# Neighbourhood attention on one core: softmax sums from columns of ones beside the values, two heads to a bank, in the slot of the logits

## The chip, the cores and the metric

The kernel runs on one core of a Trainium2 chip. The metric is the device time in microseconds (us) of one execution. TensorE (PE in the profile; PEld for its weight loads) multiplies matrices into banks of PSUM; VectorE (DVE), ScalarE (ACT) and GpSimd (POOL) work on elements; SyncE (SP) issues the DMA transfers. Every engine works through its own queue of instructions, and semaphores hold one engine back for another.

## The reference, cut to what matters

The input x is 4 images of 128 channels and 64 x 64 pixels. The program is a layer 0 and a layer 1; the change is in the attention of layer 0. Cut to what matters:

```python
y = layernorm_over_channels(x); y = y + depthwise_conv3x3(y)
# windows of 16 x 16 pixels: 64 of them; 2 branches, 4 heads of 32 channels
q, k, v = Wq @ y, Wk @ y, Wv @ y                 # per window, branch and head
logits = q . k over the 5 x 5 neighbours of each pixel * 32 ** -0.5
attn = softmax(logits)                           # out-of-window neighbours are zeros: logit 0, value 0
x = x + (Wo[0] @ o[0] + 0.5 * Wo[1] @ o[1]) / rect      # o = attn-weighted sum of v
# layer 1, over 4096 tokens of 128 channels
t = t + causal_linear_attention(layernorm(t))
t = t + recurrence(layernorm(t))                 # y_t = sigmoid(BN(W x)_t + V y_(t-1))
```

The softmax needs, for each query, a sum of exponentials of its logits (with a constant added for neighbours outside the window, `pad_c`), and the sum of values weighted by these exponentials. Their quotient is o.

## The kernel before

The image is cut into 16 bands of 16 rows (4 in each of 4 images), a band into 4 windows, so there are 64 windows, `places`. A loop runs over 66 slots. Slot i computes the logits of window i and has six gaps, 0 to 5, into which pieces of two other jobs are put by `between(i, gap)`: one step of `behind` (layer 1 of an earlier band: a list of 24 steps, `order`, one a gap over four slots, begun in slot 4m+5 for band m) and one step of `ahead` (`front()`: layer norm and depthwise convolution of the next band; in a slot that opens a band only in gaps 0, 2 and 4). `in_order()` fixes each engine's instructions in the order in which the code writes them, so that a waiting instruction holds up everything later on its engine.

What a slot holds, by lines of the profile:

- `logits` (L377, L382): four banks, one a head. Masks are added by a bf16 product. The keys of a head lie on 32 partitions, so four heads run in four row tiles of the array. ACT then writes four tiles of exponentials, `es` (L391, 128 keys by 512 queries of both branches).
- `weighted`, for the window of the slot before: (L400) for each head a product of 128x32 ones with `es`, on column tiles of 32, gives the sums in 128 rows of a bank; ACT copies them (`den`, L403), a DMA folds four rows into a 128x16 tile `dc` (L405). (L412) 24 products of values (128 keys by 32 channels) and a span of `es`, over 2 branches and 3 blocks of rows, give the weighted values of four heads in one bank; ACT copies them (`o_sb`, L420). DVE adds the constant and takes reciprocals (L423, L425); they go to DRAM (`rd`, L429) and come back broadcast over the 32 channels of each head (`rden`, L431).
- `window_inputs`, for the next window: q, k (L337) and v (L350) from `y2w`, the convolved half band of two windows; ACT copies each. v is needed with three different sets of 128 keys; the middle one is put together by two DMAs (L359, L360).
- `scaled`, for the window before last: POOL multiplies `o_sb` by `rden` into `oT` (L440), which `output0` of layer 1 multiplies by Wo (L465).

The order in a slot is: logits(i), gap 0, scaled(i-2), sums of window i-1, gap 1, values of i-1, gap 2, reciprocals, q of i+1, gap 3, k, gap 4, v, gap 5.

`convolve` gives `y2w` for two windows: ACT makes the first tap (L286), DVE the other eight (L288), ACT copies the result into window order (L324). In `front()` this copy for the first half of band n+1 falls in gap 0 of slot 4n+3, that for the second half in gap 0 of slot 4n+4. (In the first band it is made earlier by three steps.)

Tiles in a pool with one buffer (`p1`) can't be written again before their last reader is done; pools `p2` and `p3` have two and three buffers. PSUM's eight banks are used in turn.

After the 66 slots the rest of layer 1 runs out, and the recurrence follows as a chain of 43 steps (L771 to L823).

Of the kernel before, what the change touches and what calls it, by code (L numbers as in the profile page):

```python
# [9 lines left out]
F32 = mybir.dt.float32  # L10
# [7 lines left out]
P = 128  # L18
# [3 lines left out]
NB = H // WS  # L22
WT = WS * WS
# [23 lines left out]
def conv_attn_hybrid(ctx: ExitStack, tc: tile.TileContext, ins: dict, out: bass.AP):  # L47
    nc = tc.nc
# [100 lines left out]
    for i in range(2):  # L149
        t = const.tile([P, 4, P + 1], F32, name=f"v1_{i}")  # L150
        nc.vector.memset(t, 1.0)
        v1s.append(t)

    stats = const.tile([P, B * T // 512, 6], F32, name="stats")

# [20 lines left out]
    def bank():  # L176
        return ps.tile([P, 512], F32, tag="bank", name="bank")

    def run(g):
        for _ in g:  # L180
            pass
# [148 lines left out]
    def window_inputs(w, n, wj):  # L330


        y2 = y2s[n, wj // 2][:, wj % 2, :]
        for name, wT in (("q", wqT), ("k", wkT)):
            pps = bank()
            for br in range(BR):
                nc.tensor.matmul(  # L337
                    pps[:, br * WT : (br + 1) * WT],
                    wT[:, br * P : (br + 1) * P],
                    y2,  # L340
                    start=True,
                    stop=True,
                )
            w[name] = p2.tile([P, BR * WT], F32, tag=name, name=name)
            nc.scalar.copy(w[name], pps)  # L345
            yield
        vps = bank()
        v_sb = p2.tile([P, 3, BR * P], F32, tag="v_sb", name="v_sb")
        for e in range(2):
            nc.tensor.matmul(  # L350
                vps[:, e * 256 : (e + 1) * 256],
                y2[:, e * P : (e + 1) * P],
                wvT,
                start=True,
                stop=True,
            )
        nc.scalar.copy(v_sb[:, 0::2, :], vps.rearrange("p (e t) -> p e t", e=2))  # L357

        nc.sync.dma_start(v_sb[:64, 1, :], v_sb[64:, 0, :])  # L359
        nc.sync.dma_start(v_sb[64:, 1, :], v_sb[:64, 2, :])  # L360
        w["v"] = v_sb
        yield

    pieces = [(br, n) for br in range(BR) for n in range(len(BLOCKS))]
# [1 line left out]
    def spans(br, n):  # L366
        r0, r1, key0 = BLOCKS[n]
        return slice(br * WT + r0 * WS, br * WT + r1 * WS), br * WT + key0 * WS

    def logits(w):  # L370


        sps = [bank() for _ in range(HEADS)]
        for h in range(HEADS):
            rows = slice(h * HD, (h + 1) * HD)

            nc.tensor.matmul(sps[h], mask_k[rows], mask_q[rows], start=True, stop=False)  # L377
        for br, n in pieces:
            cols, k0 = spans(br, n)
            for h in range(HEADS):  # L380
                rows = slice(h * HD, (h + 1) * HD)
                nc.tensor.matmul(  # L382
                    sps[h][:, cols],
                    w["k"][rows, k0 : k0 + P],
                    w["q"][rows, cols],
                    start=False,
                    stop=(br, n) == pieces[-1],
                )
        for h in range(HEADS):
            es = p2.tile([P, BR * WT], F32, tag=f"es{h}", name=f"es{h}")  # L390
            nc.scalar.activation(es, sps[h], AF.Exp, scale=scale)  # L391
            w["es", h] = es

    def weighted(w):


        ops, dps = bank(), bank()
        for h in range(HEADS):
            rows = slice(h * HD, (h + 1) * HD)
            nc.tensor.matmul(dps[rows], ones[:, :HD], w["es", h], start=True, stop=True)  # L400

        den = p1.tile([P, BR * WT], F32, tag="den", name="den")
        nc.scalar.copy(den, dps)  # L403
        dc = p2.tile([P, 16], F32, tag="dc", name="dc")
        nc.sync.dma_start(dc, den[::HD, :])  # L405
        yield
        for br, n in pieces:
            cols, _ = spans(br, n)
            for h in range(HEADS):
                rows = slice(h * HD, (h + 1) * HD)  # L410
                c0 = br * P + h * HD
                nc.tensor.matmul(  # L412
                    ops[rows, cols],
                    w["v"][:, n, c0 : c0 + HD],
                    w["es", h][:, cols],
                    start=(br, n) == pieces[0],
                    stop=(br, n) == pieces[-1],
                )
        o_sb = p2.tile([P, BR * WT], F32, tag="o_sb", name="o_sb")
        nc.scalar.copy(o_sb, ops)  # L420
        yield

        nc.vector.tensor_tensor(dc, dc, pad_c, ALU.add)  # L423
        rc = p2.tile([P, 16], F32, tag="rc", name="rc")
        nc.vector.reciprocal(rc, dc)  # L425
        nc.vector.tensor_tensor(dmax, dmax, dc, ALU.max)
        nc.vector.tensor_tensor(dmin, dmin, dc, ALU.min)
        rd = dram4.tile([HEADS, BR * WT], F32, tag="rd", name="rd")
        nc.sync.dma_start(rd.rearrange("h (a e) -> (h a) e", e=16), rc)  # L429
        rden = p1.tile([P, BR * WT], F32, tag="rden", name="rden")  # L430
        nc.sync.dma_start(rden, rd.unsqueeze(1).to_broadcast([HEADS, HD, BR * WT]))  # L431
        w["o"], w["rden"] = o_sb, rden
        yield

# [173 lines left out]
    def layer1(n, last):  # L608

        a, c = Half(n, 0), Half(n, 1)  # L610
        y, z = last
        order = [
            (keep, z), None,
            (norm, z), (product, y), None,
            (output0, a), (measure, a), None,
            (turn_last, z), None,
            (norm, a), (output0, c), (measure, c), None,
            (turn, a), None,
            (product, z), (norm, c), None,
            (queries, a), None,  # L620
            (keys, a), None,
            (turn, c), None,
            (values, a), None,
            (queries, c), None,
            (scores, a), None,
            (keys, c), None,
            (turn_keys, a), None,
            (values, c), None,
            (accumulate, a), None,
            (turn_keys, c), None,  # L630
            (attend, a, 0), None,
            (attend, a, 1), (measure, a), None,
            (scores, c), (keep, a), None,
            (accumulate, c), (norm, a), None,
            (attend, c, 0), None,
            (turn_last, a), (attend, c, 1), (measure, c), None,
        ]
        for what in order:
            if what is None:
                yield  # L640
            elif what[1] is not None:
                what[0](*what[1:])
        halves[n] = a, c
# [17 lines left out]
    def front():  # L661


        for n in range(1, len(bands)):
            yield from norm_rows(n)
            if bands[n][1]:
                yield
            yield from convolve(n, 0)
            yield
            if n == 1:  # L670

                for _ in range(3):
                    yield
            yield from convolve(n, 1)
# [12 lines left out]
    windows = {0: {}}  # L687
    run(window_inputs(windows[0], 0, 0))
    run(third)
    ahead, behind = front(), iter(())  # L690

    def between(i, gap):


        next(behind, None)
        if i < len(places) and (i == 0 or i % NB or gap in (0, 2, 4)):
            next(ahead, None)

    for i in range(len(places) + 2):
        if i < len(places):  # L700
            n, wj = places[i]
            if i and wj == 0 and n + 1 < len(bands) and bands[n + 1][1] < NB - 1:
                load_head(n + 2)
            logits(windows[i])
        if 2 <= i:
            m, wjm = places[i - 2]
            if wjm == NB - 1:
                run(behind)
                behind = layer1(m, halves.pop(m - 1, (None, None)))
        between(i, 0)  # L710
        if 2 <= i:
            scaled(m, wjm, windows.pop(i - 2))
        if i < len(places) and wj == 1 and n + 2 < len(bands):
            load(n + 2)
        sums = weighted(windows[i - 1]) if 1 <= i <= len(places) else iter(())
        for gap in (1, 2):
            next(sums, None)
            between(i, gap)
        run(sums)
        if i == 0:  # L720
            run(fourth)
        inputs = iter(())
        if i + 1 < len(places):
            windows[i + 1] = {}
            inputs = window_inputs(windows[i + 1], *places[i + 1])
        for gap in (3, 4, 5):
            next(inputs, None)
            between(i, gap)
        run(inputs)
    run(behind)  # L730
    run(layer1_end(*halves.pop(len(bands) - 1)))
    in_order()
# [782 lines left out]
```

## Time and profile before

| | |
|---|---|
| time | 934.3 us, median of 3 (933.74 to 934.84) |
| span of the profiled run | 930.9 us |
| PE, PEld, DVE, ACT, POOL busy | 876.9, 656.1, 741.1, 539.1, 262.4 us |
| logits (L382): first and last start | 24.2 and 799.0 us |
| L400, sums: PE busy | 69.1 us, 512 instructions |
| L412, values: PE busy | 70.1 us, 3072 instructions |
| L391, exponentials: ACT busy | 132.2 us, 256 of 603 ns |
| L440, scaled: POOL busy | 86.6 us, 64 of 1354 ns |
| mean granted TensorE clock | 0.975 |

An f32 product is two instructions, so that 24 products of a window are 48 rows and 64 windows 3072. "PE busy" counts time in which at least one matmul is in flight; the mean of one matmul is its own latency, so a group in which several run side by side has far less busy time than count times mean. A row such as "x <- y" after a bar names the idle time ahead of the group and who ended it. Starts in the timeline are us from the start of the span.

### The profile page before, as it was taken

Reading aid. Unit: us, or ns where it says so; the run is one execution under the profiler, and the core shown is the slowest. Engines: PE = TensorE matmul, PEld = TensorE weight load, DVE = VectorE, ACT = ScalarE, POOL = GpSimd, SP = SyncE. Lnnn points to the kernel's source line nnn. Section 1 sums busy time; section 2 is a strip of 40 time slices with the busy share of each in tenths; the row PEclk is TensorE's granted clock in tenths of the full one; section 3 lists DMA queues with packets and bytes.
Section 4 is the critical chain, followed back from the end, with each engine's and each line's share of the span. In section 5 each row is a group of like instructions: output and inputs, shape, how many; then the busy total and the mean of one; then the engine's idle time right before and its main releaser. Section 6 shows DMA issues by size and latency. Waiting matters only on the chain.

```text
span 930.9 us, 26534 instructions
## 1 busy us (share of the span) xinstructions
PE 876.9 (94%) x10508; PEld 656.1 (70%) x10508; DVE 741.1 (80%) x2452; ACT 539.1 (58%) x1010; POOL 262.4 (28%) x359
## 2 busy tenths in 40 slices
PE   4978999999999999999999999999999999987985
PEld 3756777877777777777787777787777777755442
DVE  6464978888897988797988888798878786676886
ACT  3755566565756565656656575656566665422552
POOL 2122131413232322313041323232232312121184
PEclk9988999999999999999999999999999999988897
DMA  4111121121222121212121121212121111102853
GB/s 121 34 44 56 47 72 37 54 57 57 59 63 59 49 57 50 69 49 73 37 56 57 52 59 60 62 48 62 48 66 48 49 37 60 43 24 73 345 205 129
DMA packets 53045, 63.46 MB, mean 68 GB/s; under 512 B 22960, under 2 KB 33840, under 8 KB 52400
## 3 DMA queue, kind: packets, MB, share of 16 engines
q1 hardware_dynamic: 51184, 56.91, 19.8%
q10 hardware_dynamic: 1728, 4.77, 1.3%
q8 instruction: 85, 1.39, 0.6%
q14 instruction: 48, 0.39, 0.1%
HBM read 35.44 MB, written 17.30 MB: 57 GB/s over the span
## 4 chain that ended last, share of the span: by engine, by line
PE 60%; DVE 26%; issue 4%; ACT 4%; DMA 3%; POOL 3%; ACTq 0%; SPq 0%; DVEq 0%; POOLq 0%
DVE y L288 8%; PE bank L337 8%; PE bank L465 6%; PE bank L382 6%; PE bank L212 6%; PE bank L494 5%; PE bank L400 4%; PE bank L350 4%; PE bank L412 4%; PE bank L602 3%; DVE st L191 2%; PE bank L815 2%; PE bank L537 2%; PE bank L573 2%; DVE state L562 2%
## 5 line engine op out<-in xcount | busy, mean ns | idle before, releaser
L288 DVE SCALAR_TENSOR_TENSOR y<-ypad,cpe_w,y 128x512 f32<-128x512 f32 x240 | 189.8, 791 | 15.1 <-ACT y L286 11.7
L391 ACT ACTIVATE es<-bank 128x512 f32<-128x512 f32 x256 | 132.2, 603 | 77.1 <-PE bank L382 77.1
L440 POOL TENSOR_TENSOR oT<-o_sb,rden 128x512 f32<-128x512 f32 x64 | 86.6, 1354 | 243.1 <-DMA rden<-rd 165.8
L195 POOL TENSOR_SCALAR rs<-mv 128x4 f32<-128x4 f32 (+2 forms) x100 | 25.1, 251 | 364.4 <-DVE mv L193 163.2
L203 DVE TENSOR_SCALAR xn<-x,mv,rs 128x128 f32<-128x128 f32 x256 | 90.8, 416 | 26.5 <-POOL rs L196 26.5
L196 POOL TENSOR_TENSOR rs<-rs,mhalf 128x4 f32<-128x4 f32 (+2 forms) x100 | 106.2, 1062 | 8.3
L382 PEld LDWEIGHTS bank<-q,k 32*128 32x128 f32 x3072 | 97.7, 189 | 7.8 <-ACT k L345 6.6
L382 PE MATMUL bank<-q,k 32*128 32x96 f32 (+1 forms) x3072 | 96.3, 270 | 1.1 <-ACT k L345 1.1
L412 PEld LDWEIGHTS bank<-es,v_sb 128*32 128x32 f32 x3072 | 56.8, 110 | 30.2 <-issue 18.6
L465 PE MATMUL bank<-woT,oT 128*128 128x128 f32 x512 | 68.1, 289 | 5.7 <-POOL oT L440 5.7
L465 PEld LDWEIGHTS bank<-woT,oT 128*128 128x128 f32 x512 | 64.8, 202 | 9.7 <-POOL oT L440 7.3
L412 PE MATMUL bank<-es,v_sb 128*32 128x96 f32 (+1 forms) x3072 | 70.1, 240 | 0.0
L494 PE MATMUL bank<-xl,awT 128*128 128x512 f32 x128 | 70.0, 630 | 0.0
L400 PE MATMUL bank<-es,ones 128*32 128x512 f32 x512 | 69.1, 612 | 0.0
L357 ACT COPY v_sb<-bank 128x512 f32<-128x512 f32 x64 | 37.5, 586 | 53.5 <-PE bank L350 42.2
L337 PE MATMUL bank<-y2w,wqT 128*128 128x256 f32 x256 | 66.4, 382 | 1.0 <-DVE y2w L288 1.0
L337 PE MATMUL bank<-y2w,wkT 128*128 128x256 f32 x256 | 65.8, 380 | 0.0
L350 PE MATMUL bank<-wvT,y2w 128*128 128x256 f32 x256 | 65.8, 380 | 0.0
L345 ACT COPY q<-bank 128x512 f32<-128x512 f32 x64 | 37.6, 587 | 41.3 <-PE bank L337 39.2
L345 ACT COPY k<-bank 128x512 f32<-128x512 f32 x64 | 37.3, 583 | 36.8 <-PE bank L337 36.7
L191 DVE BATCH_NORM_STATS2 st<-x 128x6 f32<-128x128 f32 x256 | 55.5, 280 | 1.1
L337 PEld LDWEIGHTS bank<-y2w,wqT 128*128 128x128 f32 x256 | 45.8, 194 | 12.8 <-issue 7.2
(124 smaller groups left out, 1728.4 us busy)
## 6 DMA issues: line engine op xcount, KB each, us to landing
rden<-rd SPq DMA_DIRECT2D x64, 256.0 KB
v_sb<-v_sb SPq DMA_DIRECT2D x128, 64.0 KB
resd<-rs_o SPq DMA_DIRECT2D x32, 256.0 KB
out<-ot SPq DMA_DIRECT2D x32, 256.0 KB
xin<-in_xt SPq DMA_DIRECT2D x15, 512.0 KB
res<-resd SPq DMA_DIRECT2D x2, 2048.0 KB
res<-resd ACTq DMA_DIRECT2D x2, 2048.0 KB
dc<-den SPq DMA_DIRECT2D x64, 8.0 KB
```

Source lines behind the costliest of these rows:

```text
L196: nc.gpsimd.tensor_tensor(rs[:, :n], rs[:, :n], mhalf[:, :n], ALU.pow)
L203: nc.vector.tensor_scalar(xn[:, j, :], piece, mv[:, j, 0:1], rs[:, j : j + 1], ALU.subtract, ALU.mult)
L288: nc.vector.scalar_tensor_tensor(y2, src, cpe_w[:, tap : tap + 1], y2, ALU.mult, ALU.add)
L337: nc.tensor.matmul(pps[:, br * WT : (br + 1) * WT], wT[:, br * P : (br + 1) * P], y2, start=True, stop=True,)
L350: nc.tensor.matmul(vps[:, e * 256 : (e + 1) * 256], y2[:, e * P : (e + 1) * P], wvT, start=True, stop=True,)
L382: nc.tensor.matmul(sps[h][:, cols], w["k"][rows, k0 : k0 + P], w["q"][rows, cols], start=False, stop=(br, n) == pieces[-1],)
L391: nc.scalar.activation(es, sps[h], AF.Exp, scale=scale)
L400: nc.tensor.matmul(dps[rows], ones[:, :HD], w["es", h], start=True, stop=True)
L412: nc.tensor.matmul(ops[rows, cols], w["v"][:, n, c0 : c0 + HD], w["es", h][:, cols], start=(br, n) == pieces[0], stop=(br, n) == pieces[-1],)
L440: nc.gpsimd.tensor_tensor(oTs[n][:, :, :, wj * WS : (wj + 1) * WS], w["o"].rearrange("p (a r c) -> p a r c", a=BR, c=WS), w["rden"].rearra ...
L465: nc.tensor.matmul(yps[:, j * P : (j + 1) * P], oT[:, br, t], woT[:, br, :], start=br == 0, stop=br == BR - 1,)
L494: nc.tensor.matmul(zps, awT[:, m * P : (m + 1) * P], h.xl, start=True, stop=True)
```

## The change

The values get columns of ones beside them: `vt` holds, for each of 3 key sets, 2 branches and 4 heads, 32 columns of values, with 32 columns of ones between neighbours. A product with 64 of these columns gives 32 rows of weighted values and 32 rows of sums at once. Two heads fill a bank of 128 rows, so two banks (a pair of heads each) replace the bank of sums and the bank of values. In heads 0 and 3 the values land in the rows where `o_sb` wants them; heads 1 and 2 are copied into a second tile `o_mid`, with the values on rows 32 to 95, and a DMA puts these rows into `o_sb`. The sums are folded into `dc` by three small DMAs. The weighting is moved into the slot of its own logits, so one buffer of `es` is enough, and the queries and keys of the next window go into gaps 0 and 1; `scaled` follows one slot earlier; in layer 1 `output0` comes earlier in the order. The purpose is to read the exponentials once instead of twice.

The order in a slot is now: logits(i), reciprocals of i-1, gap 0, q of i+1, gap 1, k, gap 2, first pair of i, gap 3, second pair of i, gap 4, scaled(i-1), v of i+1, gap 5.

```diff
--- before.py
+++ after.py
@@ -151,6 +151,13 @@
         nc.vector.memset(t, 1.0)
         v1s.append(t)
 
+
+    vts = []
+    for i in range(2):
+        t = const.tile([P, 1 + 6 * BR * HEADS, HD], F32, name=f"vt{i}")
+        nc.gpsimd.memset(t, 1.0)
+        vts.append(t)
+
     stats = const.tile([P, B * T // 512, 6], F32, name="stats")
 
     wx = const.tile([P, B, NH, SEG, HSEGS], F32, name="wx")
@@ -345,7 +352,7 @@
             nc.scalar.copy(w[name], pps)
             yield
         vps = bank()
-        v_sb = p2.tile([P, 3, BR * P], F32, tag="v_sb", name="v_sb")
+        vt = vts[(n * NB + wj) % 2]
         for e in range(2):
             nc.tensor.matmul(
                 vps[:, e * 256 : (e + 1) * 256],
@@ -354,11 +361,15 @@
                 start=True,
                 stop=True,
             )
-        nc.scalar.copy(v_sb[:, 0::2, :], vps.rearrange("p (e t) -> p e t", e=2))
-
-        nc.sync.dma_start(v_sb[:64, 1, :], v_sb[64:, 0, :])
-        nc.sync.dma_start(v_sb[64:, 1, :], v_sb[:64, 2, :])
-        w["v"] = v_sb
+        low, mid, high = (slice(1 + 16 * k, 17 + 16 * k) for k in range(3))
+        nc.scalar.copy(
+            vt[:, 1:, :].rearrange("p (e k) d -> p e k d", e=3)[:, 0::2, 0::2],
+            vps.rearrange("p (e k d) -> p e k d", e=2, d=HD),
+        )
+
+        nc.sync.dma_start(vt[:64, mid, :], vt[64:, low, :])
+        nc.sync.dma_start(vt[64:, mid, :], vt[:64, high, :])
+        w["v"] = vt
         yield
 
     pieces = [(br, n) for br in range(BR) for n in range(len(BLOCKS))]
@@ -387,38 +398,40 @@
                     stop=(br, n) == pieces[-1],
                 )
         for h in range(HEADS):
-            es = p2.tile([P, BR * WT], F32, tag=f"es{h}", name=f"es{h}")
+            es = p1.tile([P, BR * WT], F32, tag=f"es{h}", name=f"es{h}")
             nc.scalar.activation(es, sps[h], AF.Exp, scale=scale)
             w["es", h] = es
 
+
+
+    PAIRS = (((0, 0, True), (64, 3, False)), ((0, 1, False), (64, 2, True)))
+
     def weighted(w):
 
-
-        ops, dps = bank(), bank()
-        for h in range(HEADS):
-            rows = slice(h * HD, (h + 1) * HD)
-            nc.tensor.matmul(dps[rows], ones[:, :HD], w["es", h], start=True, stop=True)
-
-        den = p1.tile([P, BR * WT], F32, tag="den", name="den")
-        nc.scalar.copy(den, dps)
+        o_sb = p2.tile([P, BR * WT], F32, tag="o_sb", name="o_sb")
+        o_mid = p1.tile([P, BR * WT], F32, tag="o_mid", name="o_mid")
+
         dc = p2.tile([P, 16], F32, tag="dc", name="dc")
-        nc.sync.dma_start(dc, den[::HD, :])
-        yield
-        for br, n in pieces:
-            cols, _ = spans(br, n)
-            for h in range(HEADS):
-                rows = slice(h * HD, (h + 1) * HD)
-                c0 = br * P + h * HD
-                nc.tensor.matmul(
-                    ops[rows, cols],
-                    w["v"][:, n, c0 : c0 + HD],
-                    w["es", h][:, cols],
-                    start=(br, n) == pieces[0],
-                    stop=(br, n) == pieces[-1],
-                )
-        o_sb = p2.tile([P, BR * WT], F32, tag="o_sb", name="o_sb")
-        nc.scalar.copy(o_sb, ops)
-        yield
+        for pair, o in zip(PAIRS, (o_sb, o_mid)):
+            ops = bank()
+            for br, n in pieces:
+                cols, _ = spans(br, n)
+                for r0, h, values_first in pair:
+                    k = 1 + 2 * ((n * BR + br) * HEADS + h) - (not values_first)
+                    nc.tensor.matmul(
+                        ops[r0 : r0 + 2 * HD, cols],
+                        w["v"][:, k : k + 2, :].rearrange("p i d -> p (i d)"),
+                        w["es", h][:, cols],
+                        start=(br, n) == pieces[0],
+                        stop=(br, n) == pieces[-1],
+                    )
+            nc.scalar.copy(o, ops)
+            if o is o_sb:
+                nc.sync.dma_start(dc[:HD], o[HD : HD + 1, :])
+                nc.sync.dma_start(dc[3 * HD :], o[2 * HD : 2 * HD + 1, :])
+            else:
+                nc.sync.dma_start(dc[HD : 3 * HD], o[0 : 3 * HD + 1 : 3 * HD, :])
+            yield
 
         nc.vector.tensor_tensor(dc, dc, pad_c, ALU.add)
         rc = p2.tile([P, 16], F32, tag="rc", name="rc")
@@ -429,6 +442,8 @@
         nc.sync.dma_start(rd.rearrange("h (a e) -> (h a) e", e=16), rc)
         rden = p1.tile([P, BR * WT], F32, tag="rden", name="rden")
         nc.sync.dma_start(rden, rd.unsqueeze(1).to_broadcast([HEADS, HD, BR * WT]))
+
+        nc.sync.dma_start(o_sb[HD : 3 * HD], o_mid[HD : 3 * HD])
         w["o"], w["rden"] = o_sb, rden
         yield
 
@@ -611,10 +626,10 @@
         y, z = last
         order = [
             (keep, z), None,
+            (output0, a), (measure, a), None,
             (norm, z), (product, y), None,
-            (output0, a), (measure, a), None,
-            (turn_last, z), None,
-            (norm, a), (output0, c), (measure, c), None,
+            (output0, c), (measure, c), None,
+            (turn_last, z), (norm, a), None,
             (turn, a), None,
             (product, z), (norm, c), None,
             (queries, a), None,
@@ -687,7 +702,7 @@
     windows = {0: {}}
     run(window_inputs(windows[0], 0, 0))
     run(third)
-    ahead, behind = front(), iter(())
+    ahead, behind, sums = front(), iter(()), iter(())
 
     def between(i, gap):
 
@@ -707,26 +722,30 @@
             if wjm == NB - 1:
                 run(behind)
                 behind = layer1(m, halves.pop(m - 1, (None, None)))
-        between(i, 0)
-        if 2 <= i:
-            scaled(m, wjm, windows.pop(i - 2))
-        if i < len(places) and wj == 1 and n + 2 < len(bands):
-            load(n + 2)
-        sums = weighted(windows[i - 1]) if 1 <= i <= len(places) else iter(())
-        for gap in (1, 2):
-            next(sums, None)
-            between(i, gap)
         run(sums)
-        if i == 0:
-            run(fourth)
-        inputs = iter(())
+        inputs, sums = iter(()), iter(())
         if i + 1 < len(places):
             windows[i + 1] = {}
             inputs = window_inputs(windows[i + 1], *places[i + 1])
-        for gap in (3, 4, 5):
-            next(inputs, None)
-            between(i, gap)
+        if i < len(places):
+            sums = weighted(windows[i])
+        between(i, 0)
+        next(inputs, None)
+        if i < len(places) and wj == 1 and n + 2 < len(bands):
+            load(n + 2)
+        between(i, 1)
+        next(inputs, None)
+        between(i, 2)
+        if i == 0:
+            run(fourth)
+        next(sums, None)
+        between(i, 3)
+        next(sums, None)
+        between(i, 4)
+        if 1 <= i <= len(places):
+            scaled(*places[i - 1], windows.pop(i - 1))
         run(inputs)
+        between(i, 5)
     run(behind)
     run(layer1_end(*halves.pop(len(bands) - 1)))
     in_order()
```

## The prediction

> **What bounds the kernel now.** I read the engine shares first, then the stretches of the middle, then the two groups that the change merges, then one slot in order of time, and last the waits.
>
> The engine row of the page, and one line of the table of stretches (length, then busy us of PE, PEld, DVE, ACT, POOL, clock, DMA share, GB/s):
>
> ```profile
> PE 876.9 (94%) x10508; PEld 656.1 (70%) x10508; DVE 741.1 (80%) x2452; ACT 539.1 (58%) x1010; POOL 262.4 (28%) x359
> 420.00:520.00 100.00, 99.30 (x1280) 75.36 (x1279) 85.60 (x285) 62.00 (x113) 27.69 (x37) 1.00 0.20 57
> ```
>
> From about slot 6 to slot 63 TensorE is never idle and its clock is whole. There a removed matmul is worth its streaming time, and a new wait of TensorE is lost in full. DVE at 86% comes close behind.
>
> The groups that the change merges, and two rows of weight loads:
>
> ```profile
> L412 PEld LDWEIGHTS bank<-es,v_sb 128*32 128x32 f32 x3072 | 56.8, 110 | 30.2 <-issue 18.6
> L382 PEld LDWEIGHTS bank<-q,k 32*128 32x128 f32 x3072 | 97.7, 189 | 7.8 <-ACT k L345 6.6
> L400 PE MATMUL bank<-es,ones 128*32 128x512 f32 x512 | 69.1, 612 | 0.0
> L412 PE MATMUL bank<-es,v_sb 128*32 128x96 f32 (+1 forms) x3072 | 70.1, 240 | 0.0
> ```
>
> The reader is to see busy time against count times mean. 512 x 612 ns is 313 us, yet the row covers 69.1: four column tiles of 32 run side by side. So do the values (3072 x 240 ns = 737 against 70.1).
>
> The timeline around slot 31, which makes the inputs of the next band's first window (start, us, engine, line):
>
> ```profile
> 397.57 1.48 PE L382 MATMUL bank<-q,k 32*128 32x96 f32 x48
> 398.98 1.16 PE L537 MATMUL bank<-f,f 128*128 128x128 f32 x8
> 399.08 2.07 ACT L391 ACTIVATE es<-bank 128x512 f32<-128x512 f32 x4 [0.94 <-PE bank L382]
> 400.07 1.06 PE L400 MATMUL bank<-es,ones 128*32 128x512 f32 x8
> 400.39 0.74 DVE L288 SCALAR_TENSOR_TENSOR y<-ypad,cpe_w,y 128x512 f32<-128x512 f32 x1
> 401.07 1.12 PE L494 MATMUL bank<-xl,awT 128*128 128x512 f32 x2
> 401.17 0.62 ACT L324 COPY y2w<-y 128x512 f32<-128x512 f32 x1
> 402.12 1.09 PE L412 MATMUL bank<-es,v_sb 128*32 128x96 f32 x48
> 403.14 0.66 PE L529 MATMUL bank<-ident,f 128*128 128x128 f32 x4
> 403.64 1.03 PE L337 MATMUL bank<-y2w,wqT 128*128 128x256 f32 x4
> ```
>
> The sums take 1.00 us from start to next start (400.07 to 401.07), the values 1.02. The copy of y2w stands behind the four exponentials on ACT and ends at 401.79; the query product that reads it starts at 403.64, with 1.85 us to spare.
>
> The reciprocals' broadcast in the same slot, and three rows of the waits (total, times, longest):
>
> ```profile
> 399.01 0.57 SPq L431 DMA_DIRECT2D rden<-rd  x1
> 403.87 1.28 POOL L440 TENSOR_TENSOR oT<-o_sb,rden 128x512 f32<-128x512 f32 x1 [11.48 <-DMA rden<-rd]
> PE bank L465 <- POOL oT L440: 5.7, 5, 2.6
> PE bank L212 <- DVE xn L203: 4.8, 5, 2.5
> PE bank L337 <- DVE y2w L288: 1.0, 1, 1.0
> ```
>
> The broadcast lands 4.9 us after its issue. Little of TensorE's time is waiting: these rows are most of it.
>
> **What the Trainium skill says.** "TensorEngine Tiling (Array Packing)", Available Configurations: with 128 rows, 32-wide tiles are four, 64-wide tiles two. The four are in this trace; the two are not, as no 64-wide tile runs. The same page, Key Properties, says that a change of tiling mode drains TensorE. The trace agrees: values right behind sums cost 0.89 us (41.26 to 42.15), with a full-array stage behind them 1.0. "TensorE: Matmul & The Clock Gate", LDWEIGHTS, prices a load by its columns over 1.2 in ns: 107 for 128, 53 for 64, 27 for 32. L382 fits: 12 rounds of four in 1.41 us are 117 ns, near the 107. The same page, Architectural detail, has ACT and DVE as strict FIFO, which the order of exponentials and y2w above shows.
>
> **The change part by part.**
>
> *Matmuls.* Removed per window: the sums, 1.00 us. The values, 1.02 us, become two pair stages of 24 instructions on 64-wide tiles. Each streams 512 columns in two passes over two tiles, the time of the old stage over four. A round loads 128 columns of weights before and after. Lower bound 1.02 us a stage. If a tile's load of 53 ns can't be quite hidden behind its 64-column matmuls (53 ns; 80 at 96, from 0.86 us over 1,024 columns), rounds of 63 instead of 53 ns, after L382's 10 ns over its price, add 0.03. The upper bound has the loads of two tiles one after another: 12 x 107 + 160 ns = 1.44. I take 1.04: 2.08 against 2.02, 64 windows, **+3 us**. So the sums aren't free: they only use tiles that the values now give up.
>
> *ACT.* A copy of den goes, a copy of o_mid comes, both 128x512 (L403 613 ns, L420 599). The scattered write of v is the same size. Nothing.
>
> *The query product moves up.* It now follows gap 0. In slots 4n+3, y2w is copied in that gap. TensorE has only scores (L537, to 399.97 here) between the logits and the product, but ACT must finish four exponentials (401.15) and the copy (401.79), and about 0.1 us passes on. Wait 1.9 us here; at 499.87 scores start and y2w ends at 502.53, giving 1.8. The last tap on DVE ends at 401.13, so DVE doesn't help. Key product, pair stages and all the rest of TensorE's queue stand behind this wait. Slots 7, 11 to 59 are 14 (in slot 3 the copy was made a slot earlier): 14 x 1.8 = **+25 us**.
>
> *Layer 1's order.* Both output0 come earlier, turn_last follows norm z by two gaps as before. But norm a now comes on DVE behind the addition and measurement of c. After c's output0 DVE needs 0.15 + 0.69 + 0.87 + 0.36 + 1.15 = 3.2 us to the end of norm a (L472, L191, L193, L203); TensorE has a pair stage 1.02, turn_last 0.6, values 0.87 = 2.5, and its four transposes overlap in part. About 0.5 us in 15 bands, less some of the 4.8 waited there before: **+4**.
>
> *DMA and the single buffers.* One more transfer a window (o_mid into o_sb, 128 KB) is queued behind rden; two more small dc transfers. ACT's copy into o_mid waits for the preceding transfer, as o_mid has one buffer; v's copy and the next exponentials are queued behind. From DVE's reciprocal: rd to rden 1.6 (397.35 to 399.01), landing 4.9, o_mid perhaps 0.5 more, copy 0.75, dc 1.9 (38.25 to 40.16), DVE 0.5: a loop of 10.2 us. A slot in the middle is 11.2 to 14.2 (logits at 385.74, 397.35, 408.55, 422.76, 436.17), mean 12.6, so the loop fits, and ACT's wait of 0 to 2 us lies beside TensorE's gaps 4 and 5 and the values: **+2**, range 0 to 20. es with one buffer is read to the end two gaps before the next logits: nothing. POOL's filling of vts lies in its idle time between 1.62 and 6.87, before the first load's statistics.
>
> *Start.* Slots 1 to 4 are 6.4 us now and the loop is 10.2. But slot 5 stalls today: logits wait 4.4 us at 63.84, output0 starts at 76.06 having waited for oT. Following the loop by hand I reach slot 6 at 86 us against 84.5, with one weighted stage (2 us) more done: 0.
>
> *End.* The last output0 starts at 821.12, after oT at 819.81, itself behind rs (818.84) on POOL. Now the last window's scaled stands before that rs, and 2 us of sums and values have moved out of slot 64: output0 near 817, -4. The 5.7 us of L465 waits mostly go, as oT is ready some gaps earlier: -2. **-6 us.**
>
> Sum: 3 + 25 + 4 + 2 - 6 = +28; 934.3 + 28 = **962 us**.
>
> **The rivals.**
> 1. *Faster, 14%.* The y2w wait is absorbed because everything behind it runs ahead meanwhile, and end, oT and transposes give 9: 925 us. For: the scaling is ready earlier. Against: TensorE is at 99%, so there's no slack to absorb anything, and the ACT order is fixed. Sums wholly saved would be 934 - 64 = 870; the overlap of L400 with itself speaks against.
> 2. *Even, 5%.* Waits and gains are equal: 934.
> 3. *The loop through o_mid is the bound, 8%.* If the landing is 3 us longer (in 384.18 to 390.9, beside an xin load, it was 6.7), the loop is 13.2, and some 45 slots of 58 stretch by about 1.4: +63, 25 of it in place of the y2w wait: about 1000.
> 4. *64-wide loads don't overlap, 7%.* 2 x 64 x 0.42 = 54 more less the 3: 1013.
>
> The forecast, slower by some 10 to 45 us, has 66%.
>
> **How the numbers follow.** Slower is forecast plus rivals 3 and 4, 0.81; faster 0.14; same 0.05. The range, 930 to 998, holds the forecast, the even case and a part of rival 1, and the weaker forms of rival 3; outside are the rest of 1, and 4.
>
> **What would show it.** Right: pair stages at 1.02 to 1.07 us from start to start; a wait of the first query product for ACT's y2w, about 14 times 1.8 us; TensorE below 98% in the middle; rows of the middle slots 4n+3 longer by 2 us. Wrong: pair stages near 1.4 or near 0.5; no wait at the query product; ACT's o_mid copy waiting over 3 us in most slots with logits behind it.

## The result, and the profile after

The changed kernel takes 977.4 us (median of 4, 972.2 to 980.8) against 934.6 (933.7 to 938.5): the ratio is 1.0445, with an interval of 1.0389 to 1.0501. It is 43 us slower; 28 were forecast. 977.4 lies inside the stated range of 930 to 998.

Line numbers have moved. The two stages L400 and L412 are now one line, L421; logits L382 is L393, the exponentials L391 are L402, the query and key products L337 are L344, the copy of y2w L324 is L331, output0 L465 is L480, scaled L440 is L455, the transposes L212 are L219.

The page after the change, engine shares, and the same 100 us of the table of stretches (length, then busy us of PE, PEld, DVE, ACT, POOL, clock, DMA share, GB/s):

```profile
PE 892.4 (91%) x9996; PEld 713.0 (73%) x9996; DVE 756.5 (77%) x2452; ACT 544.3 (56%) x1010; POOL 251.4 (26%) x361
420.00:520.00 100.00, 95.39 (x1159) 79.10 (x1159) 83.73 (x278) 58.49 (x106) 26.30 (x38) 1.00 0.26 76
```

TensorE was busy for 99.3 of these 100 us and is now busy for 95.4. It has 512 instructions fewer and more busy time: the sums were not saved, and about 4% of the middle is waiting.

The merged groups, after:

```profile
L421 PEld LDWEIGHTS bank<-es,vt 128*64 128x64 f32 x3072 | 120.7, 138 | 40.0 <-ACT k L352 16.7
L421 PE MATMUL bank<-es,vt 128*64 128x96 f32 (+1 forms) x3072 | 145.3, 244 | 4.6 <-DMA vt<-vt 4.6
```

69.1 + 70.1 us of busy time have become 145.3. The mean of one matmul is the same (244 ns against 240), with half as many side by side.

TensorE's waits after the change (total, times, longest):

```profile
PE bank L344 <- ACT y2w L331: 23.4, 14, 2.1
...
PE bank L219 <- DVE x L602: 6.8, 14, 0.8
PE bank L219 <- DVE xn L210: 5.8, 5, 2.5
PE bank L421 <- DMA vt<-vt: 4.6, 3, 2.6
...
PE bank L480 <- POOL oT L455: 3.0, 1, 3.0
```

The first row wasn't there before in this form. It comes 14 times.

The timeline around slot 31, the one that the prediction shows for the kernel before (start, us, engine, line):

```profile
422.21 1.48 PE L393 MATMUL bank<-q,k 32*128 32x96 f32 x48
423.62 1.16 PE L552 MATMUL bank<-f,f 128*128 128x128 f32 x8
423.78 2.07 ACT L402 ACTIVATE es<-bank 128x512 f32<-128x512 f32 x4 [1.00 <-PE bank L393]
425.44 0.74 DVE L295 SCALAR_TENSOR_TENSOR y<-ypad,cpe_w,y 128x512 f32<-128x512 f32 x1
426.22 0.62 ACT L331 COPY y2w<-y 128x512 f32<-128x512 f32 x1 [0.37 <-DVE y L295]
426.89 1.13 PE L344 MATMUL bank<-y2w,wqT 128*128 128x256 f32 x4 [2.11 <-ACT y2w L331]
```

The query product starts 0.05 us after the copy ends. Between the scores' start at 423.62 and the product at 426.89 lie 3.27 us, of which the scores need 1.0. In this slot DVE's last tap (to 426.18) ends a little after the exponentials (425.85), as in slot 15; in slot 47 both end together. In the other 11 the exponentials come last, and the tap has ended 0.2 to 1.0 us before the copy begins. While TensorE waits, nothing behind it in its queue can go.

The two pair stages of slot 30 (from a listing of TensorE alone, start and us):

```profile
416.49 1.11 PE L421 MATMUL bank<-es,vt 128*64 128x96 f32 x24
417.54 0.66 PE L219 MATMUL bank<-ident,xn 128*128 128x128 f32 x4
418.13 1.11 PE L421 MATMUL bank<-es,vt 128*64 128x96 f32 x24
419.17 1.16 PE L526 MATMUL bank<-awT,xl 128*128 128x128 f32 x8
```

From start to next start they take 1.05 and 1.04 us, where the sums took 1.00 and the values 1.02.

### The profile page after: what moved, and what is told of

Its sections match the earlier page's. It is cut to its first block, busy times and chain, and to the rows that moved or that the text cites. A ratio compares the mean times of both kernels' runs of the same rounds, so it can differ in the third digit from the quotient of the medians.

```text
span 976.5 us, 26069 instructions
## 1 busy us (share of the span) xinstructions
PE 892.4 (91%) x9996; PEld 713.0 (73%) x9996; DVE 756.5 (77%) x2452; ACT 544.3 (56%) x1010; POOL 251.4 (26%) x361
## 4 chain that ended last, share of the span: by engine, by line
PE 66%; DVE 17%; DMA 6%; ACT 5%; issue 3%; POOL 1%; ACTq 0%; SPq 0%; DVEq 0%; POOLq 0%
PE bank L421 11%; PE bank L344 9%; PE bank L219 7%; PE bank L480 6%; PE bank L393 6%; DVE y L295 6%; PE bank L509 6%; PE bank L357 4%; PE bank L526 3%; PE bank L617 3%; DMA res<-resd 2%; ACT es L402 2%; PE bank L588 2%; PE bank L569 2%; DVE st L198 2%
## 5 line engine op out<-in xcount | busy, mean ns | idle before, releaser
L295 DVE SCALAR_TENSOR_TENSOR y<-ypad,cpe_w,y 128x512 f32<-128x512 f32 x240 | 209.4, 872 | 12.6 <-ACT y L293 8.6
L402 ACT ACTIVATE es<-bank 128x512 f32<-128x512 f32 x256 | 132.3, 604 | 76.7 <-PE bank L393 76.7
L455 POOL TENSOR_TENSOR oT<-o_sb,rden 128x512 f32<-128x512 f32 x64 | 85.7, 1339 | 325.8 <-DMA rden<-rd 311.4
L421 PEld LDWEIGHTS bank<-es,vt 128*64 128x64 f32 x3072 | 120.7, 138 | 40.0 <-ACT k L352 16.7
L421 PE MATMUL bank<-es,vt 128*64 128x96 f32 (+1 forms) x3072 | 145.3, 244 | 4.6 <-DMA vt<-vt 4.6
L203 POOL TENSOR_TENSOR rs<-rs,mhalf 128x4 f32<-128x4 f32 (+2 forms) x100 | 99.5, 995 | 8.3
L393 PEld LDWEIGHTS bank<-q,k 32*128 32x128 f32 x3072 | 96.8, 187 | 1.1
L393 PE MATMUL bank<-q,k 32*128 32x96 f32 (+1 forms) x3072 | 94.7, 268 | 0.0
L344 PE MATMUL bank<-y2w,wqT 128*128 128x256 f32 x256 | 71.3, 403 | 24.4 <-ACT y2w L331 23.4
L210 DVE TENSOR_SCALAR xn<-x,mv,rs 128x128 f32<-128x128 f32 x256 | 82.7, 386 | 1.4 <-POOL rs L203 1.4
L428 ACT COPY o_mid<-bank 128x512 f32<-128x512 f32 x64 | 37.5, 585 | 74.3 <-PE bank L421 71.9
L344 PEld LDWEIGHTS bank<-y2w,wqT 128*128 128x128 f32 x256 | 46.3, 197 | 38.8 <-ACT y2w L331 26.0
L365 ACT COPY vt<-bank 128x512 f32<-128x512 f32 x64 | 37.5, 587 | 62.1 <-PE bank L357 60.8
L480 PE MATMUL bank<-woT,oT 128*128 128x128 f32 x512 | 65.5, 282 | 3.1 <-POOL oT L455 3.0
L480 PEld LDWEIGHTS bank<-woT,oT 128*128 128x128 f32 x512 | 62.2, 195 | 6.6 <-POOL oT L455 3.6
L344 PE MATMUL bank<-y2w,wkT 128*128 128x256 f32 x256 | 67.0, 385 | 0.0
L513 DVE TENSOR_SCALAR low<-low 128x512 f32<-128x512 f32 x64 | 26.9, 421 | 48.3 <-ACT low L511 48.3
L344 PEld LDWEIGHTS bank<-y2w,wkT 128*128 128x128 f32 x256 | 47.7, 195 | 19.2 <-issue 11.7
L487 DVE TENSOR_TENSOR x<-bank,xin 128x512 f32<-128x512 f32 x32 | 22.1, 691 | 47.3 <-PE bank L480 47.3
```

Of the source, the lines that this page charges most:

```text
L203: nc.gpsimd.tensor_tensor(rs[:, :n], rs[:, :n], mhalf[:, :n], ALU.pow)
L210: nc.vector.tensor_scalar(xn[:, j, :], piece, mv[:, j, 0:1], rs[:, j : j + 1], ALU.subtract, ALU.mult)
L295: nc.vector.scalar_tensor_tensor(y2, src, cpe_w[:, tap : tap + 1], y2, ALU.mult, ALU.add)
L344: nc.tensor.matmul(pps[:, br * WT : (br + 1) * WT], wT[:, br * P : (br + 1) * P], y2, start=True, stop=True,)
L393: nc.tensor.matmul(sps[h][:, cols], w["k"][rows, k0 : k0 + P], w["q"][rows, cols], start=False, stop=(br, n) == pieces[-1],)
L421: nc.tensor.matmul(ops[r0 : r0 + 2 * HD, cols], w["v"][:, k : k + 2, :].rearrange("p i d -> p (i d)"), w["es", h][:, cols], start=(br, n) ...
```

## The experiments

The question was which part costs: the order of the slot (with the wait for y2w), the order in layer 1, or the merge itself (wider tiles, columns of ones, o_mid and its transfer). All times are medians; "before" was 934.0, 933.9 and 934.0 us in the three sets of runs.

### The query and key products later

```diff
         between(i, 0)
-        next(inputs, None)
...
         between(i, 1)
-        next(inputs, None)
         between(i, 2)
...
+        next(inputs, None)
         next(sums, None)
         between(i, 3)
+        next(inputs, None)
         next(sums, None)
```

> The changed kernel, with the queries of the next window after gap 2 and its keys after gap 3 instead of after gaps 0 and 1; nothing else. If the wait of the first query product for the y2w copy is the main cost (14 times 1.9 us, and three dips of the clock behind it worth some 5 us): the row of this wait disappears, and the time falls from 977 to about 945 (938 to 952). If the merged matmuls, the o_mid transfer or the single buffers are the cost: the time stays above 968.

959.1 us (958.1 to 959.7), ratio 1.0272 (1.0245 to 1.0298). Half of an answer: 18 us of the 32 expected. Two of TensorE's waits in this run:

```profile
PE bank L219 <- DVE x L602: 15.8, 15, 1.3
...
PE bank L344 <- ACT y2w L331: 4.5, 14, 0.3
```

The y2w wait fell from 23.4 to 4.5 us, but the transposes of keep(a), in slots 4n, now wait for DVE for 15.8 us instead of 6.8: TensorE seems to come to that step earlier, and DVE not. So the product's place is a real cost, and part of what is won comes back as another wait.

### The order alone

The changed kernel with the `weighted` and the value copies of the kernel before (separate `ones` and values, `den`, `v_sb`); loop, layer 1 order and single `es` buffer as changed.

```diff
-        for pair, o in zip(PAIRS, (o_sb, o_mid)):
...
+        ops, dps = bank(), bank()
+        for h in range(HEADS):
+            rows = slice(h * HD, (h + 1) * HD)
+            nc.tensor.matmul(dps[rows], ones[:, :HD], w["es", h], start=True, stop=True)
...
```

> The changed kernel's order and single buffer of exponentials, but the sums and values as separate matmuls as before (no columns of ones, no o_mid, no transfer into o_sb). If the order is the cost: about 972 (965 to 979), as two stages of 1.00 and 1.02 us replace two of 1.045, 4 us less. If the merge is the cost: about 940.

969.1 us (965.7 to 972.0), ratio to before 1.0376 (1.0337 to 1.0416). The order without the merge makes most of the loss; the merge adds 8 us to it. The wait is there without a column of ones in the program:

```profile
PE bank L338 <- ACT y2w L325: 24.1, 14, 2.2
```

### Order alone, products later

The two edits above together.

> Separate sums and values in the changed kernel's order, with queries after gap 2 and keys after gap 3. If wait and merge are independent: 4 us under the kernel with merged matmuls and later queries, about 941, and near the kernel before (934.6) up to the new order of layer 1. If the merge matters more than by its stage time, it is more than 10 us under it.

954.9 us (948.9 to 956.3), ratio 1.0206 (1.0161 to 1.0250): 4 under the merged kernel with later products, as forecast for independent costs, but 14 above the 941 named, which had been worked out from the 945 expected of that kernel. The wait for DVE's x (16.7 us, against 3.1 before) is of the size of these 14 us, so "near the kernel before" was wrong for this order.

### Values right behind the sums, in the kernel before

```diff
         nc.sync.dma_start(dc, den[::HD, :])
-        yield
         for br, n in pieces:
...
         nc.scalar.copy(o_sb, ops)
         yield
+        yield
```

> The kernel before, with the values right behind the sums (gap 1 after both), so that two stages with the same tiles follow each other. If a change of tile width costs TensorE about 0.12 us, as the difference of 0.89 and 1.00 us from start to start says: 64 times 0.12 is 7.7, so about 927. If that difference is only modelled ends in the trace: 934, no change.

934.7 us (932.0 to 936.5), ratio 1.0008 (0.9992 to 1.0024). The time says "no change", yet the stages did become shorter. Summed over the trace from each matmul's start to the next one's:

```
us, all 64 windows             sums    values   transposes of keep
kernel before                  64.1     69.1      25.5
values right behind sums       57.3     63.8      41.0
```

12 us are saved, 8.7 of them in the 57 windows after the first 100 us. So two stages with the same tiles in a row do take less: the sums, with the values right behind them, 0.88 instead of 1.00 us, and the values 1.00 instead of 1.02. (The prediction's 0.89 us is such a stage of sums too, not one of values.) But 15.5 us are given back at keep(a). Its wait in the kernel before, and in this run:

```profile
PE bank L212 <- DVE x L587: 3.1, 10, 0.6
...
PE bank L212 <- DVE x L587: 16.7, 15, 1.4
```

Read this way, the kernel before is held by two engines: TensorE, always busy, and DVE in the slots 4n (13.5 of 14.2 us busy in slot 32). Taking work from TensorE alone gained nothing here; a wait added to it can still be lost in the slots where DVE has slack (9.8 of 11.2 us busy in slot 31).

### Moving what waits, and what DVE does there

The transposes of keep(a) two gaps later, first with the values behind the sums, then alone:

```diff
-            (scores, c), (keep, a), None,
+            (scores, c), None,
             (accumulate, c), (norm, a), None,
-            (attend, c, 0), None,
+            (attend, c, 0), (keep, a), None,
```

> The kernel before with the values right behind the sums, as in the run that changed nothing, and the transposes of keep(a) moved from the step of scores(c) to that of attend(c, 0), two gaps later. In the run that changed nothing TensorE saved 12 us in the two stages and gave 15 back waiting for DVE's x at keep(a). If that wait is what ate the gain: about 923 (918 to 928). If DVE itself bounds the slot, the wait moves to another matmul: 931 to 936.

> The kernel before with keep(a) two gaps later and nothing else. If its wait at keep(a), about 0.5 us in 14 bands, is lost time: 928. If DVE bounds the slot: 934, as before.

939.6 us (ratio 1.0084, 1.0053 to 1.0115) and 934.4 us (1.0011, 0.9997 to 1.0024). No gain, and the first is above both of its forecasts: the wait moved to the next matmuls that need DVE. In the first of them:

```profile
PE bank L573 <- DVE aT L539: 8.8, 8, 1.3
PE bank L575 <- DVE state L562: 8.8, 14, 0.7
```

Then one scaling step of the front, 1.1 us of DVE, out of the slots 4n:

```diff
-        if i < len(places) and (i == 0 or i % NB or gap in (0, 2, 4)):
+        if i < len(places) and (i == 0 or i % NB or gap in (0, 2)):
             next(ahead, None)
+        if 1 < i < len(places) and i % NB == 1 and gap == 3:
+            next(ahead, None)
```

> The kernel before with the values right behind the sums, and one step of the front (the scaling of the next band's first rows, 1.1 us of DVE) moved from gap 4 of each slot 4n into gap 3 of slot 4n+1, which then has two. If DVE's work in slots 4n is what took back the 12 us that TensorE saved: that slot shortens by about 0.8 us in 14 bands, so about 923. If DVE's backlog comes from earlier slots anyway, or slot 4n+1 now waits: 932 to 938.

941.6 us, ratio 1.0092 (1.0067 to 1.0116). This too is above both forecasts, and the edit couldn't test what it was meant to: the step stood in gap 4, and keep(a) waits in gap 2, so nothing that DVE does ahead of the wait in its slot became less. The wait for x is 18.1 us, and output0 now waits for oT 12 times instead of 6 (10.7 us against 7.3). Whether less DVE work ahead of gap 2 would free the 12 us wasn't tried, so DVE as the second bound is read from the traces; no run shows it by taking work from DVE there.

### The first half's convolution a gap earlier

In the changed kernel, for 11 of the 14 bands (a band that opens an image has a step more and keeps its wait):

```diff
-            if bands[n][1]:
-                yield
             yield from convolve(n, 0)
             yield
+            if bands[n][1]:
+                yield
```

> The changed kernel with the first half's convolution one gap earlier in 11 of the 14 bands concerned, so that its y2w copy stands on ACT ahead of the exponentials of slot 4n+3; queries stay after gap 0. If the place of the copy behind the exponentials makes the wait: 11 of 14 waits vanish, with their clock dips 20 to 28 us, so 950 to 958, less what the slots 4n give back at keep(a). If DVE's taps are the limit: the wait is as long, and the time 972 to 980.

955.6 us (951.5 to 962.5), ratio 1.0226 (1.0189 to 1.0264): 21.8 less, for 11 waits. The three that remain:

```profile
PE bank L219 <- DVE xn L210: 11.0, 15, 2.5
...
PE bank L344 <- ACT y2w L331: 5.4, 3, 2.1
```

With the copy ahead of the exponentials on ACT, the wait is gone, though the product still stands after gap 0. So the cost is that y2w comes too late for that place, and not the product as such. But the run doesn't separate the two things that make y2w late, as its expectation took it to, because DVE's taps moved up with the copy: in slot 11 the last tap ends 3.1 us after the slot's first matmul in the changed kernel, and 1.4 us after it here. In the 11 waits that went, the last tap had ended 0.57 us before the copy, in the mean. With the exponentials out of the way and the taps where they were, about 1.0 of the 1.6 us of each wait would have stayed (an estimate from these ends). In the three that remain the tap comes last in two and within 0.3 us of the copy in the third. A part comes back as transposes waiting for xn (11.0 against 5.8 us).

### Layer 1's old order

```diff
             (keep, z), None,
-            (output0, a), (measure, a), None,
             (norm, z), (product, y), None,
-            (output0, c), (measure, c), None,
-            (turn_last, z), (norm, a), None,
+            (output0, a), (measure, a), None,
+            (turn_last, z), None,
+            (norm, a), (output0, c), (measure, c), None,
```

> The changed kernel with layer 1's steps in the order of the kernel before. If norm(a) behind the measurement of c costs what the transposes wait there (0.37 us in most bands, some 5 us): about 972. If the earlier output0 gains more at the end than this costs: 980 or more.

968.1 us (967.0 to 973.1), ratio 1.0393 (1.0354 to 1.0433), 9 less. By start to next start, the transposes of xn take 7.3 us less, and the matmuls from the logits to product(z) 2.7 less. The second part I hadn't seen: with the new order POOL's reciprocal root for c is queued ahead of the copies that pad the next band's rows, ACT's first tap waits for these copies, and the exponentials, the copy of xl and product(z) queue behind it. The two waits in the changed kernel, slot 14:

```profile
194.98 0.81 ACT L293 ACTIVATE y<-ypad,cpe_b,cpe_w 128x512 f32<-128x512 f32 x1 [5.25 <-POOL ypad L281]
196.80 1.12 PE L617 MATMUL bank<-xl,fwT 128*128 128x512 f32 x2 [0.83 <-ACT xl L612]
```

ACT sat idle for 5.25 us and TensorE for 0.8; slots 14, 30 and 46 last 12.5 us instead of 11.6.

### Both, with and without the merge

> The changed kernel with both the first half's convolution a gap earlier and layer 1's old order. If the two costs are separate (22 and 9 us): about 946. If the wait only moves: 952 or more.

946.1 us (945.5 to 947.2), ratio 1.0141 (1.0114 to 1.0168): 31.3 less than the changed kernel, the two gains of 21.8 and 9.3 added.

The same with the sums and values of the kernel before:

> As the kernel with both costs taken away, but with separate sums and values instead of columns of ones. If the merge costs its stage time only (0.07 us a window): 4 to 6 us under it, about 941. If o_mid, its transfer and the wider values cost more: 12 us or more under it, near 934.

934.8 us (930.5 to 941.6; 20 runs), ratio 1.0012 (0.9997 to 1.0027). So the merge costs 11.3 us here, where nothing else differs, and the rest of the new order, with three of its waits still in it, is level with the kernel before. Two pairs of runs above differ by the merge alone as well: there it costs 8.3 us (977.4 against 969.1) and 4 us (959.1 against 954.9), so its price depends on what stands around it. By start to next start the stages take 143.4 us with the merge and 130.1 without. Of these 13.3 us, 5.8 are waits for the middle values in a few early slots; 5.4 fall in the 57 windows after the first 100 us, most of it the stage time, two of 1.045 against 1.00 and 1.02; the rest is in the first slots. The wait with the merge, and without:

```profile
PE bank L421 <- DMA vt<-vt: 5.8, 4, 3.7
...
PE bank L415 <- DMA v_sb<-v_sb: 0.2, 1, 0.2
```

There the slots are short (about 8 us), and the values' transfer has to land before the pairs of the very next slot. Three things differ with the merge: this transfer is twice as large with the ones in it (128 KB against 64 for each half), the first pair needs the values at once, where the sums had stood ahead of them, and the transfers out of o_mid go through the same queue. Which of them makes the wait isn't shown.

### Two buffers of o_mid

```diff
-        o_mid = p1.tile([P, BR * WT], F32, tag="o_mid", name="o_mid")
+        o_mid = p2.tile([P, BR * WT], F32, tag="o_mid", name="o_mid")
```

> The changed kernel with two buffers of o_mid. If ACT's wait for the transfer out of o_mid is hidden, as forecast: 977 within the scatter (970 to 981). If the loop through o_mid holds slots up: 965 or less.

979.3 us (975.0 to 980.8), ratio to the kernel before 1.0487 (1.0453 to 1.0520): not faster than the changed kernel, and the first slots aren't shorter either (63.1 us from slot 0 to slot 6, against 63.3). In the changed kernel ACT's copy into o_mid waits for TensorE, not for the transfer:

```profile
ACT o_mid L428 <- PE bank L421: 71.9, 58, 1.8
```

## Why the prediction was right, and where its sum was short

The forecast was slower by 28; it is 43. The main mechanism was right: the first query product waits for y2w 14 times, nothing absorbs it, and the largest term has about the right size. Two terms make the sum short: the merge (3 forecast, 4 to 11 in three pairs of runs) and layer 1's order (4 forecast, 9 measured). With the convolution earlier, layer 1's old order and no merge the kernel is back at 934.8: 21.8, 9.3 and 11.3 us are nearly all of the 43.

One half of the reading of the bound failed: that "a removed matmul is worth its streaming time". With the values behind the sums TensorE's stages took 12 us less, and the time stayed at 934.7. The prediction shows three rows of waits and calls them most of TensorE's; they are 11.5 of 46 us. The row of keep(a), 3.1 us, wasn't among them, and it is the one that grew when TensorE got faster.

By its steps:

- *Matmuls, +3.* Stages of 1.04 us were forecast, 1.04 and 1.05 are there (0.06 us in 64 windows are 3.8, put down as 3). Four column tiles had hidden the sums, and two tiles of twice the width have no more room: "the sums aren't free" holds. The two bounds (loads wholly hidden, or one after another at 1.44) are decided for the first. The price of 53 ns for a load doesn't show in the trace, where one of 64 columns lasts 138 ns; but 24 of them, 3.3 us, fit into a stage of 1.04, so they overlap. What the Trainium skill states in "TensorEngine Tiling (Array Packing)", Available Configurations, that there are two tiles where they are 64 wide, could be checked only now, and the trace agrees: a product on the full array streams 1,024 columns in 0.86 us from start to next start (L344, 412.96 to 413.82), a pair stage 2,048 in 1.04, so two 64-wide tiles do run side by side. That the merge as a whole costs more comes in good part from the start.
- *The query product, +25.* 14 waits, 23.4 us in the profile's own count, and 21.8 us of time for the 11 taken away. "DVE doesn't help" was too short a reading: its taps end within about 1 us of the exponentials, in two slots after them, and the runs don't separate the two. The sum left out the clock, which in this profile drops behind three of the waits (some 5 us, told below).
- *Start, 0.* Too small. Slot 6 begins at 89.6 us against 84.5 before; 86 were forecast. 2.3 us of this are there at slot 0 already (26.2 against 24.0), but slot 0 began at 23.4 in the run with two buffers, where nothing ahead of it differs. From slot 0 to slot 6 it is 63.3 us against 60.5 before, and 58.9 with the order alone: the merge adds 4.5 there (6.0 in the pair at 946.1 and 934.8). The prediction's account of the start doesn't mention the values' transfer, and TensorE's waits for it (4.6 and 5.8 us) are of this size. Besides, the 2 us of weighting that moved from the end to the start are credited twice, in this 0 and in the -4 of the end.
- *Layer 1's order, +4.* Clearly mis-sized: taking it back gains 9 us. DVE's chain from output0(c) to norm(a) was priced rightly in kind, but the transposes behind it take 7.3 us more, and POOL's order (2.7 us) was not followed: the bands that open an image pad their rows one gap later, behind the reciprocal root for c.
- *DMA and single buffers, +2.* The run with two buffers shows no gain to be had from the single one; the loop of 10.2 us fits in the slots of the middle.
- *End, -6.* From the last logits (slot 63) to the end it was 133.4 us and is 130.7. 2 us of this are the weighting that no longer stands behind them, so little else was gained. The waits for oT went from 5.7 to 3.0, where "mostly go" was forecast.

The rivals: rival 1 (the wait absorbed) falls, since all 14 waits are there at full length, and rival 2 (even) by the time. Rival 3 (the loop through o_mid) falls by the run with two buffers. Rival 4 (loads that don't overlap) falls by the stages of 1.04.

What stays open: how much of the y2w wait is ACT's queue and how much DVE's taps; which part of the merge makes the waits at the start; and what the clock's drops add, as their number differs from profile to profile (none to five in the middle) and no experiment isolates them.

## What to carry to other kernels

Narrow matmuls on column tiles are cheap in company: before two are merged into a wider one, compare the columns that each tile streams before and after, as merged columns may only take the tiles that its neighbours were using. When a consumer is moved up in a queue, follow its producer through that engine's own queue: here a 0.6 us copy, queued behind four exponentials and fed by DVE's taps, cost more than the merge of the matmuls. And on a core where two engines are near full, a saving on one shows up as its wait for the other; measure the edit, not the stage.

## What was not expected of the hardware

A wait of 1.6 to 2.1 us was at times followed by a slower TensorE. Four of the slots 4n+3 of the changed kernel, from the table of stretches (the last but two columns: the granted clock):

```profile
152.57:165.80 13.23, 11.61 (x151) 9.73 (x154) 9.99 (x20) 7.73 (x14) 1.28 (x1) 1.00 0.19 52
206.79:221.80 15.01, 13.17 (x147) 10.62 (x146) 10.67 (x21) 7.80 (x14) 2.80 (x2) 0.89 0.17 46
261.06:275.95 14.89, 13.27 (x147) 10.59 (x147) 10.24 (x23) 7.70 (x14) 1.58 (x1) 0.89 0.17 47
475.60:488.80 13.20, 11.58 (x147) 9.70 (x147) 9.95 (x21) 7.70 (x14) 1.28 (x1) 1.00 0.19 52
```

The four do the same work behind nearly the same wait, and two of them last 1.7 us longer at a mean clock of 0.89. In this profile it happens three times in the middle, in slots 15, 19 and 51, some 5 us in all; in the profile of the kernel before the granted clock is whole from 80 to 820 us. The spread of the times says nothing on this: the four runs of the changed kernel spread by 0.9%, and 27 of the kernel before as much.

All kept profiles together show a pattern, though not its cause. In each of the 14 the clock changes only at whole multiples of 3.413 us from one another. Cut into stretches of this length, the middles (from slot 6 to the last logits) hold 44 in which TensorE sat idle for 1.55 us or more by the profile's (modelled) ends, and 18 of these were followed by a stretch at half clock. Of 67 with 1.0 to 1.55 us idle one was, and of 2862 with less none. What sets the 18 apart from the other 26 isn't shown.
